# An audio tower with attention and a phase-table FFN: a ring of up to eight sequences in place of fixed quads, and softmax sums and squares on VectorE

## Chip, cores and metric

The kernel runs on one core of a Trainium2 chip. The metric is device time in microseconds. In this text PE is TensorE (PEld its weight loads), ACT is ScalarE, DVE is VectorE, POOL is GpSimd and SP is the engine that issues the DMAs.

## What is computed

The input is 32 signals, each cut into 313 frames of 512 samples. A DCT makes h; then come one attention layer and one FFN layer, each with a layernorm ahead and a residual around it. Everything is float32. Cut to what matters:

```python
h = frames @ D.T                                   # (32, 313, 512)
h = h + attn(layernorm(h))
h = h + ffn(layernorm(h))

# attn, 8 heads of 64
Q, K, V = rotate(X @ W_Q), rotate_inverse(X @ W_K), X @ W_V
p = softmax(Q @ K.T) * gamma_h ** abs(n - m)
Y = groupnorm(p @ V)                               # one group for each head
out = (silu(X @ W_G) * Y) @ W_O

# ffn, 256 units n, 512 features d
theta = x[..., None, :] / (1 + abs(W)) + B_param   # (32, 313, 256, 512)
idx = mod(round(theta * 4096 / (2 * pi)), 4096)
cos_sum = sum_d(cos_table[idx] * attn_cos)         # (32, 313, 256)
sin_sum = sum_d(sin_table[idx] * attn_sin)
out = silu(cos_sum @ proj_cos.T + sin_sum @ proj_sin.T)
```

The FFN is by far the largest part: 32 x 313 x 256 x 512 angles, of each a sine and a cosine.

## The kernel before, in words

**FFN** (`ffn`, line 538). The eight quads of four sequences are worked off one after the other. Features lie on the 128 partitions in four chunks c, and the 4 x 313 = 1252 frames of a quad along the free dimension, so a unit has 4 x 1252 = 5008 columns. For each of the 256 units DVE makes the table index: four instructions `index` (line 556), one for each chunk, multiply xT by the unit's scale and add its bias, both read per partition, and write int16; `mask` (line 563) wraps the index. ACT takes the sine of all 5008 columns in one instruction (line 581). For the cosine DVE adds a quarter turn (`quarter`, line 568) and wraps again (`wrap`, line 574), and ACT takes a second sine. PE sums over the features with one-hot weights `hot` (line 591): four sequences go to four groups of 32 output partitions of a PSUM bank, one row for each of 32 units. After 32 units DVE copies both banks (line 603) and SP stores them to `sums_d`. There are four index buffers, three sine buffers and four PSUM banks `pa`, of which a block of 32 units uses two.

**Attention** (`attention`, line 293) works on one sequence at a time: DCT (`rows`, line 275), layernorm with its reciprocal square root on POOL (lines 234 and 226), transposes, V, the gate's projection with silu (line 324), then two halves of four heads. For each pair of heads Q and K are projected twice (`columns`, line 289) and rotated on DVE. A half makes scores (line 352) and row maxima (line 360), and subtracts them for three heads (line 369); then ACT takes the exponentials with twelve instructions (line 378), each of which also gives the sum of its row block in `accum_out`. For every head follow transposes (399), the decay (411) and the product with V (417). At the end come the group norm (square on ACT, line 440; line 444 and on), the gate, W_O, the second layernorm and the store of the transposed result to `xT_d`. Copies of h, xnT, V and the last transposed block from PSUM are on ACT (line 210, `ENG_*`). `output` (line 493) loads the FFN sums of a sequence, projects them, takes the silu (510), adds h (513) and stores.

**Order.** The order on each engine is fixed before the run by `Plan` (line 46). Each operation has a key, an engine, an estimated duration and the buffers that it reads and writes; `emit` plays the engines forward and each takes, of what is ready, the operation with the lowest key. So keys say what is due first. An FFN unit takes two keys, one for each sine; a quad takes 512. The first four attentions run before any FFN, two at a time in buffer sets A and B (the memory of B is then given to the FFN by `swap`, line 692). Later attentions are spread over the FFN of the quad before (line 704), four in 452 keys, on buffer set A:

```python
    for b in range(QUAD):
        attention(plan, lambda x: -1000.0 + b // 2 + x, 0, b, (A, B)[b % 2])
    ...
    for q in range(n_quads):
        k0 = q * SLOTS
        for b in range(QUAD if q else 0):
            output(plan, k0 + 30.0 * b / QUAD - 4.0, q - 1, b, A)
        for b in range(QUAD if q + 1 < n_quads else 0):
            attention(plan, lambda x: k0 + 30.0 + (SLOTS - 60.0) * (b + x) / QUAD, q + 1, b, A)
        ffn(plan, k0)
```

Of the kernel before, what the change touches and what calls it, by code (L numbers as in the profile page):

```python
# [12 lines left out]
F32 = mybir.dt.float32  # L13
I32 = mybir.dt.int32
# [14 lines left out]
QUAD = 4  # L29
# [10 lines left out]
ENG_H = "ACT"  # L40
ENG_XNT = "ACT"
ENG_V = "ACT"
ENG_A5 = "ACT"
# [83 lines left out]
def tile_audio_tower(ctx: ExitStack, tc: tile.TileContext, t: dict, out: bass.AP):  # L127
    nc = tc.nc
    n_quads = t["frames"].shape[0]
    S = t["frames"].shape[4]  # L130
    T = QUAD * S
# [7 lines left out]
    out_v = out.rearrange("(a b) s d -> a b s d", b=QUAD)  # L139
# [8 lines left out]

    xT_d = dram.tile([P, NC4, T], F32, name="xT_d")
    sums_d = dram.tile([2, P, 2, T], F32, name="sums_d")  # L150
    wv_d = dram.tile([NC4, P, HOP], F32, name="wv_d")
    h_d = dram.tile([n_quads, QUAD, S, HOP], F32, name="h_d")

    class Buffers:


        def __init__(self, name, pool, psum):
# [8 lines left out]
            self.a5 = sb("a5", NC4, S)  # L166
            self.h = sb("h", NT, HOP)
            self.xn = sb("xn", NT, HOP)
            self.xnT = sb("xnT", NC4, S)
            self.v = sb("v", NT, HOP)  # L170
            self.gate = sb("gate", NC4, S)
            self.qk = [sb(f"qk{i}", 2, S) for i in range(2)]
            self.raw = sb("raw", 2, S)
            self.prob = sb("prob", NB, NT, S)
            self.probT = sb("probT", NT, S)
            wide = self.prob.rearrange("p a b s -> p (a b s)")
# [105 lines left out]
    def columns(plan, key, x, bank, src):  # L282

        k = x.load(plan, key, src)

        def go():
            w = x.ring[k].rearrange("p (c n) -> p c n", n=P)
            for c in range(NC4):
                nc.tensor.matmul(x.W[:, bank, :S], w[:, c, :], x.xnT[:, c, :],  # L289
                                 start=(c == 0), stop=(c == NC4 - 1))  # L290
        plan.add(key, "PE", 2200, go, (x.k("xnT"), x.k("ring", k)), x.banks(bank))

    def attention(plan, keys, q, b, x):
# [4 lines left out]
        def step(n=1.0):  # L298
            done[0] += n
            return keys(done[0] / 139.0)  # L300

        xns, probs = x.every("xn", NT), x.every("prob", NB)
        W3 = x.W[:N, :NT, :]
        plan.add(step(0), "SP", DMA_NS, lambda: nc.sync.dma_start(x.a5, t["frames"][q, b]), (),
                 (x.k("a5"),))
        rows(plan, step(7), x, x.a5, t["dct"], (x.k("a5"),))
        copy(plan, step(), ENG_H, NT * HOP, x.h[:N], W3, x.banks(0, 1, 2), (x.k("h"),))
        layernorm(plan, step(3), x)
        transposed(plan, step(3), x)
        copy(plan, step(), ENG_XNT, NC4 * S, x.xnT, x.W[:, :, :S], x.banks(0, 1, 2, 3), (x.k("xnT"),))  # L310
# [4 lines left out]
        copy(plan, step(), ENG_V, NT * HOP, x.v[:N], W3, x.banks(0, 1, 2), (x.k("v"),))  # L315
        plan.add(step(0), "POOL", 500, lambda: nc.gpsimd.memset(x.v[0:1, : NT - 1, :], 0.0), (),
                 (x.k("v"),))


        key = step(6)  # L320
        for g in range(NC4):
            columns(plan, key, x, g, t["wg"][g])
        plan.add(step(), "ACT", 1270,
                 lambda: nc.scalar.activation(x.gate, x.W[:, :, :S], AF.Silu),
                 x.banks(0, 1, 2, 3), (x.k("gate"),))

        for hb in range(H // NB):
            for g in range(hb * NB // 2, (hb + 1) * NB // 2):
                key = step(4)
                qk = x.qk[g % 2]  # L330
                kq = x.k("qk", g % 2)
# [12 lines left out]
                plan.add(key, "DVE", 1640, turned, x.banks(2, 3), (x.k("raw"), kq))  # L344
            for hd in range(hb * NB, (hb + 1) * NB):
                key = step(2.5)
                a, r0 = hd % NB, (hd % 2) * DH
                qk, kq = x.qk[hd // 2 % 2], x.k("qk", hd // 2 % 2)
# [25 lines left out]
            def exps(hb=hb, m=m):  # L374
                for a in range(NB):
                    for i in range(NT):
                        last = a == NB - 1
                        nc.scalar.activation(  # L378
                            x.prob[:N, a, i, :],
                            x.W[:N, i, :S] if last else x.prob[:N, a, i, :], AF.Exp,  # L380
                            bias=m[:N, i : i + 1] if last else 0.0,
                            accum_out=x.sm[:N, i, hb * NB + a : hb * NB + a + 1],
                        )

                nc.scalar.activation(x.lu[:1, 0:1], x.lu[:1, 0:1], AF.Silu)
            plan.add(step(), "ACT", 8700, exps, (x.k("mx", 1), *x.banks(0, 1, 2)),
                     [*probs, x.k("sm", hb), x.k("lu")])
            for hd in range(hb * NB, (hb + 1) * NB):
# [25 lines left out]
                for i in range(NT):  # L414
# [8 lines left out]
                    plan.add(key, "PE", 1000, go, (x.k("probT"), x.k("v")), x.banks(3))  # L423
                if hd % 2 == 0:
# [9 lines left out]


# [3 lines left out]
        plan.add(key, "ACT", 1500,  # L439
                 lambda: nc.scalar.activation(x.sq[:N], x.xn[:N], AF.Square), xns, probs)  # L440
# [23 lines left out]
        for c in range(NC4):  # L464
# [6 lines left out]
                 lambda: nc.vector.tensor_tensor(x.gate, x.gate, x.aff, ALU.mult), probs,  # L471
                 (x.k("gate"),))
        rows(plan, step(7), x, x.gate, t["wo"], (x.k("gate"),))
# [3 lines left out]
        for i in range(NT):  # L477
            f0 = 1 if i else 0
            plan.add(
                step(0), "SP", DMA_NS,  # L480
                lambda i=i, f0=f0: nc.sync.dma_start(
                    h_d[q, b, ROW0[i] + f0 : ROW0[i] + N, :], x.h[f0:N, i, :]),
                (x.k("h"),), (("h_d", q, b, i),),
            )
# [7 lines left out]

    def output(plan, key, q, b, x):

        probs, xns = x.every("prob", NB), x.every("xn", NT)

        def load():
            for m in range(2):
# [328 lines left out]
```

## Time and profile before

| | us |
|---|---|
| median of 3 runs | 19201.89 (19189.18 to 19209.79) |
| profiled execution | 19200.94 |
| its span, first to last instruction | 19199.2 |
| ACT busy, of it sines (line 581) | 18323.5, 17522.7 |
| DVE busy, of it index (line 556), mask, quarter, wrap (563, 568, 574) | 17754.5, 7108.7, 9010.3 |
| PE busy, of it the FFN's sums (line 591) | 14967.9, 10546.7 |
| first sine starts | 679.7 |
| last sine ends | 19130.4 |
| granted TensorE clock, mean | 0.913 |

A group line of the profile names source line, engine, operation, output and inputs, shapes and count; after the bar stand the busy time of the group in us and the mean duration in ns, and after the second bar the idle time of the engine just before these instructions, with what ended it. Instructions of one engine overlap a little in the records, so that the busy time of a group is less than count times mean. A line of the table of stretches gives for each engine its busy us and instructions in that stretch, then the granted clock as a share of full speed, the mean share of the DMA engines and GB/s.

### The profile page before, as it was taken

Reading aid. Unit: us, or ns where it says so; the run is one execution under the profiler, and the core shown is the slowest. Engines: PE = TensorE matmul, PEld = TensorE weight load, DVE = VectorE, ACT = ScalarE, POOL = GpSimd, SP = SyncE. Lnnn points to the kernel's source line nnn. Section 1 sums busy time; section 2 is a strip of 40 time slices with the busy share of each in tenths; the row PEclk is TensorE's granted clock in tenths of the full one; section 3 lists DMA queues with packets and bytes.
Section 4 is the critical chain, followed back from the end, with each engine's and each line's share of the span. In section 5 each row is a group of like instructions: output and inputs, shape, how many; then the busy total and the mean of one; then the engine's idle time right before and its main releaser. Section 6 shows DMA issues by size and latency. Waiting matters only on the chain.

```text
span 19199.2 us, 336270 instructions
## 1 busy us (share of the span) xinstructions
PE 14967.9 (78%) x148864; PEld 6732.7 (35%) x148864; DVE 17754.5 (92%) x17005; ACT 18323.5 (95%) x6051; POOL 581.0 (3%) x1222
## 2 busy tenths in 40 slices
PE   8777777887787877888777887788787777877666
PEld 5433333333333333333333333333333333322222
DVE  3799999999999999999999999999999999999997
ACT  1699999999999999999999999999999999999998
POOL 0000000000000000000000000000000000000000
PEclk8899999999999998999989999899999999987898
DMA  3111111111121111111111111111111111110001
GB/s 92 51 40 39 40 41 59 42 42 41 34 65 40 40 42 38 58 42 43 40 57 37 42 43 41 57 41 39 39 43 61 39 40 41 39 49 17 18 18 37
DMA packets 455954, 828.47 MB, mean 43 GB/s; under 512 B 54208, under 2 KB 103360, under 8 KB 454496
## 3 DMA queue, kind: packets, MB, share of 16 engines
q1 hardware_dynamic: 454496, 806.95, 14.3%
q8 instruction: 1169, 19.15, 0.4%
q14 instruction: 289, 2.37, 0.0%
HBM read 723.64 MB, written 83.10 MB: 42 GB/s over the span
## 4 chain that ended last, share of the span: by engine, by line
ACT 36%; DVE 33%; PE 17%; issue 11%; POOL 3%; DMA 0%; DVEq 0%; ACTq 0%; SPq 0%; POOLq 0%
ACT trig L581 34%; DVE ix L556 13%; PE pa L591 11%; DVE ix L563 5%; DVE ix L568 5%; DVE ix L574 5%; PE a_W L275 2%; PE a_W L289 2%; ACT a_prob L378 1%; DVE a_mx L360 1%; PE a_W L417 1%; PE a_W L352 1%; DVE a_prob L369 1%; POOL a_lu L226 1%; DVE a_st L238 0%
## 5 line engine op out<-in xcount | busy, mean ns | idle before, releaser
L581 ACT ACTIVATE trig<-ix 128x5008 f32<-128x5008 int16 x4096 | 17522.7, 4368 | 201.0 <-DVE ix L563 132.8
L591 PE MATMUL pa<-trig,hot 128*32 128x313 f32 x131072 | 10546.7, 468 | 3449.9 <-ACT trig L581 3433.5
L591 PEld LDWEIGHTS pa<-trig,hot 128*32 128x32 f32 x131072 | 4114.7, 117 | 9466.3 <-ACT trig L581 5200.6
L556 DVE TENSOR_SCALAR ix<-xT,f_scale,f_bias 128x1252 int16<-128x1252 f32 x8192 | 7108.7, 927 | 331.0 <-ACT trig L581 326.9
L568 DVE TENSOR_SCALAR ix<-ix 128x5008 int16<-128x5008 int16 x2048 | 3006.7, 1468 | 206.5 <-ACT trig L581 15.6
L563 DVE TENSOR_SCALAR ix<-ix 128x5008 int16<-128x5008 int16 x2048 | 2999.5, 1465 | 68.3
L574 DVE TENSOR_SCALAR ix<-ix 128x5008 int16<-128x5008 int16 x2048 | 3004.2, 1467 | 61.7
L289 PE MATMUL a_W<-a_xnT,a_ring 128*128 128x313 f32 x4800 | 1402.1, 437 | 92.2 <-DVE a_qk L338 66.6
L289 PEld LDWEIGHTS a_W<-a_xnT,a_ring 128*128 128x128 f32 x4800 | 873.3, 190 | 618.3 <-issue 156.1
L275 PE MATMUL a_W<-a_ring,a_a 128*105 128x512 f32 x1488 | 700.1, 612 | 27.5 <-DMA a_ring<-in_dct 15.4
L417 PEld LDWEIGHTS a_W<-a_v,a_probT 105*105 105x105 f32 x4320 | 482.7, 188 | 316.7 <-issue 187.5
L417 PE MATMUL a_W<-a_v,a_probT 105*105 105x64 f32 x4320 | 546.2, 277 | 41.1 <-DVE a_probT L411 41.0
L352 PE MATMUL a_W<-a_qk 64*105 64x313 f32 x1440 | 481.2, 459 | 100.8 <-DVE a_prob L369 75.9
L399 PE MATMUL a_W<-ident,a_prob 105*105 105x105 f32 x2160 | 350.4, 305 | 234.2 <-ACT a_prob L378 216.4
L275 PE MATMUL a_W<-a_ring,a_gate 128*105 128x512 f32 x720 | 377.0, 643 | 70.5 <-DVE a_gate L471 70.5
L399 PEld LDWEIGHTS a_W<-ident,a_prob 105*105 105x105 f32 x2160 | 282.0, 205 | 393.8 <-ACT a_prob L378 260.9
L275 PEld LDWEIGHTS a_W<-a_ring,a_a 128*105 128x105 f32 x1488 | 241.4, 173 | 419.4 <-issue 400.7
L275 PE MATMUL a_W<-a_ring,a_xnT 128*105 128x512 f32 x720 | 354.0, 616 | 2.8 <-ACT a_xnT L210 2.8
L226 POOL TENSOR_TENSOR a_gu<-a_gr 105x24 f32<-105x24 f32 x90 | 48.5, 539 | 10147.2 <-DVE a_gr L220 10142.5
L352 PEld LDWEIGHTS a_W<-a_qk 64*105 64x105 f32 x1440 | 224.1, 173 | 361.2 <-DVE a_prob L369 146.5
L262 PE MATMUL a_W<-ident,a_xn 105*128 105x105 f32 x1080 | 177.7, 291 | 172.5 <-DVE a_xn L250 90.1
L378 ACT ACTIVATE a_prob<-a_prob 105x313 f32<-105x313 f32 x540 | 242.6, 451 | 67.2 <-DVE a_prob L369 66.5
(136 smaller groups left out, 4029.3 us busy)
## 6 DMA issues: line engine op xcount, KB each, us to landing
hot<-in_hot SPq DMA_DIRECT2D x1024, 256.0 KB
a_dec<-in_decay SPq DMA_DIRECT2D x240, 260.5 KB
a_ring<-in_proj SPq DMA_DIRECT2D x128, 256.0 KB
a_ring<-in_dct SPq DMA_DIRECT2D x120, 256.0 KB
a_ring<-wv_d SPq DMA_DIRECT2D x120, 256.0 KB
a_ring<-in_wg SPq DMA_DIRECT2D x120, 256.0 KB
a_ring<-in_wq SPq DMA_DIRECT2D x120, 256.0 KB
a_ring<-in_wk SPq DMA_DIRECT2D x120, 256.0 KB
```

The costliest lines, as they stand in the source:

```text
L275: lambda c=c, i=i, k=k, to=to: nc.tensor.matmul(x.W[:N, to, :], lhsT[:, c, ROW0[i] : ROW0[i] + N], x.ring[k], start=(c == 0), stop=(c == N ...
L289: nc.tensor.matmul(x.W[:, bank, :S], w[:, c, :], x.xnT[:, c, :], start=(c == 0), stop=(c == NC4 - 1))
L352: lambda i=i, qk=qk, r0=r0: nc.tensor.matmul(x.W[:N, i, :S], qk[r0 : r0 + DH, 0, ROW0[i] : ROW0[i] + N], qk[r0 : r0 + DH, 1, :], start=Tru ...
L378: nc.scalar.activation(x.prob[:N, a, i, :], x.W[:N, i, :S] if last else x.prob[:N, a, i, :], AF.Exp, bias=m[:N, i : i + 1] if last else 0. ...
L399: nc.tensor.transpose(x.W[:N, jj, ROW0[i] : ROW0[i] + N], x.prob[:N, a, i, ROW0[j] : ROW0[j] + N], ident[:N, :N],)
L417: nc.tensor.matmul(x.y[:N, i, (hd % 2) * DH : (hd % 2 + 1) * DH], x.probT[:N, jj, ROW0[i] : ROW0[i] + N], x.v[:N, jj, hd * DH : (hd + 1) * ...
L556: nc.vector.tensor_scalar(now["ix", x][:, c, :], now["xT", c], f_scale[:, c, n : n + 1], f_bias[:, c, n : n + 1], ALU.mult, ALU.add)
L563: nc.vector.tensor_scalar(now["ix", x], now["ix", x], LUT - 1, LUT // 2, ALU.bitwise_and, ALU.bitwise_xor)
L568: nc.vector.tensor_scalar(new("ix", y, [P, NC4, T], I16, bufs=N_IX), now["ix", x], float(LUT // 4), None, ALU.add)
L574: nc.vector.tensor_scalar(now["ix", x], now["ix", x], LUT - 1, None, ALU.bitwise_and)
L581: nc.scalar.activation(new("trig", w, [P, NC4, T], bufs=N_TRIG), now["ix", x], AF.Sin, bias=-PI32, scale=ANG)
L591: nc.tensor.matmul(now["pa", p][b * 32 : b * 32 + 32, :S], now["hot", z][:, n % 2, c, k, :], now["trig", w][:, c, b * S : (b + 1) * S], st ...
```

## The change

**Ring and rounds.** Quads give way to 16 pairs of sequences. A ring has four places of one pair each. The FFN runs in 42 rounds of 32 units; a pair joins the ring at the round in `STARTS`, stays eight rounds, in which all 256 units come by (the block of units is the round's number modulo 8), and leaves. The ring holds one pair in rounds 0 to 3, two to round 9, three to round 13, four to round 35, then three, two and one for two rounds each. In rounds 36 and 37 the three pairs lie in places 0, 2 and 3, in rounds 38 and 39 the two lie in 0 and 2.

```python
STARTS = (0, 4, 8, 10, 12, 14, 16, 18, 20, 22, 24, 26, 28, 30, 32, 34)
SLOT = 16
```

**Width of an instruction.** Units are worked on two at a time. A sine instruction takes `n_p` parts (a part is one chunk of one unit, with all r sequences of the ring): eight with two sequences, four with four, two with six or eight. So a sine, mask, quarter or wrap again has 5008 columns, and 3756 with six sequences. An index instruction covers one part and one run of adjacent places of the ring: 626 columns for each pair in the run, 2504 with a full ring. With a full ring the sums take two banks for the sine and two for the cosine, which is all four.

```diff
-            for c in range(NC4):
-                def index(x=xs, c=c, n=n):
...
-                    nc.vector.tensor_scalar(
-                        now["ix", x][:, c, :], now["xT", c],
-                        f_scale[:, c, n : n + 1], f_bias[:, c, n : n + 1], ALU.mult, ALU.add)
+        n_p = min(SLOT // r, 2 * NC4) if SLOT % r == 0 else 2
+        E = n_p * r * S
+        n_slots = 2 * NC4 // n_p
+        n_banks = -(-r // 4)
...
+                        for pt, (c, u) in enumerate(parts):
+                            for at, j, m in runs:
+                                def index(x=x, pt=pt, c=c, u=u, n=n, at=at, j=j, m=m):
...
+                                    nc.vector.tensor_scalar(
+                                        now["ix", x][:, d0 : d0 + 2 * m * S],
+                                        now["xT", c][:, 2 * at * S : 2 * (at + m) * S],
+                                        f[:, 0, c, n + u : n + u + 1], f[:, 1, c, n + u : n + u + 1],
+                                        ALU.mult, ALU.add)
```

Scales and biases of the units no longer stay in SBUF: they are stored to DRAM (`f_d`) at the start, and each round loads its block of 32, eight keys ahead. With two sequences in a bank the even and odd units go to different partition groups, and the stores to `sums_d` are split in two.

**When attention runs.** Only the first two sequences run ahead of the FFN. The other thirty are spread by keys so that each pair is done eight keys before it joins: two of 60 keys, eight of 96, twenty of 128, the last ending at key 3448 of 4096. A joining pair is loaded into its place of the ring two keys ahead of the round. Outputs are placed between attentions, and the last two come after the last round.

**Exponentials, sums and squares.** `attention` gets an argument `eng`. It is "ACT" for the first two sequences and for those that start while the ring holds one pair (sequences 2, 3 and 4), and "DVE" for the other 27. With "DVE" the copies of h, xnT, V and the last transposed block are on DVE, and:

```diff
             def exps(hb=hb, m=m):
+                if eng == "DVE":
+                    nc.scalar.activation(x.prob[:N, : NB - 1], x.prob[:N, : NB - 1], AF.Exp)
                 for a in range(NB):
                     for i in range(NT):
                         last = a == NB - 1
-                        nc.scalar.activation(
...
-                            accum_out=x.sm[:N, i, hb * NB + a : hb * NB + a + 1],
-                        )
+                        if last or eng == "ACT":
+                            nc.scalar.activation(
...
+                                accum_out=x.sm[:N, i, hb * NB + a : hb * NB + a + 1]
+                                if eng == "ACT" else None,
+                            )
...
+            for a in range(0, NB if eng == "DVE" else 0, 2):
+                plan.add(step(0), "DVE", 2120,
+                         lambda h0=hb * NB + a, a=a: nc.vector.tensor_reduce(
+                             x.sm[:N, :, h0 : h0 + 2].rearrange("p i h -> p h i"),
+                             x.prob[:N, a : a + 2], AX.X, ALU.add),
...
+            plan.add(key, "DVE", 1760,
+                     lambda: nc.vector.tensor_tensor(x.sq[:N], x.xn[:N], x.xn[:N], ALU.mult),
```

**Buffers.** One buffer `u` serves as input frames, Q and K, gate, and last transposed block; V is written over h, so h is stored to DRAM after the DCT and loaded again after the heads; the gate's projection with its silu moves from ahead of the heads to behind them; `raw` is a part of `probT`. The four matmuls of `columns` become four operations of the plan in place of one.

## Prediction, made before the changed kernel ran

> **What bounds the kernel now.** I read the page's busy line first, then a table of stretches, then the groups of one steady quad by form.
>
> ```profile
> PE 14967.9 (78%) x148864; PEld 6732.7 (35%) x148864; DVE 17754.5 (92%) x17005; ACT 18323.5 (95%) x6051; POOL 581.0 (3%) x1222
> ```
>
> ACT is busy 95% and DVE 92%, so neither share alone names a bound. The stretches (columns: length, then busy us of PE, PEld, DVE, ACT, POOL, granted clock, DMA) separate four stages:
>
> ```profile
> 0.00:320.00 320.00, 274.47 (x1018) 187.69 (x1019) 117.58 (x144) 51.42 (x121) 13.12 (x58) 0.77 0.28 86
> 320.00:680.00 360.00, 305.41 (x1136) 200.19 (x1134) 131.33 (x194) 54.21 (x124) 21.70 (x100) 0.79 0.30 90
> ...
> 5367.30:7692.20 2324.90, 1847.42 (x18609) 829.75 (x18609) 2213.13 (x2124) 2289.80 (x757) 77.58 (x152) 0.93 0.15 44
> ...
> 17060.00:19060.00 2000.00, 1331.29 (x15016) 497.00 (x15008) 1844.16 (x1656) 2000.00 (x470) 0.00 (x0) 0.85 0.06 18
> ```
>
> Up to 680 us the first four attentions run alone, two at a time, with PE 85% busy and ACT nearly empty. A steady quad (four sequences of FFN with the next four attentions inside) takes 2324.9 us, 581 a sequence, with ACT at 98.5% and DVE at 95.2%; the last quad, without attention, runs ACT without a gap. After the last sine come 69 us of four output projections. The groups of the steady quad show what fills both engines (us in the stretch, mean ns, idle before):
>
> ```profile
> L581 ACT ACTIVATE trig<-ix 128x5008 f32<-128x5008 int16 x513 | 2195.5, 4367 | 28.1 <-DVE ix L563 17.7 <-DVE ix L574 7.0 <-PE pa L591 3.5
> L378 ACT ACTIVATE a_prob<-a_prob 105x313 f32<-105x313 f32 x72 | 32.3, 451 | 0.1
> L440 ACT ACTIVATE a_prob<-a_xn 105x1536 f32<-105x1536 f32 x4 | 5.9, 1466 | 0.0
> L210 ACT COPY a_v<-a_W 105x1536 f32<-105x1536 f32 x4 | 5.7, 1426 | 0.0
> ...
> L556 DVE TENSOR_SCALAR ix<-xT,f_scale,f_bias 128x1252 int16<-128x1252 f32 x1024 | 889.0, 927 | 31.5 <-ACT trig L581 31.2
> L568 DVE TENSOR_SCALAR ix<-ix 128x5008 int16<-128x5008 int16 x256 | 376.0, 1469 | 25.8 <-ACT trig L581 2.2 <-DVE ix L563 1.4
> ...
> L360 DVE TENSOR_REDUCE a_mx<-a_W 105x3 f32<-105x939 f32 x32 | 36.1, 1129 | 0.0
> L250 DVE TENSOR_SCALAR a_xn<-a_h,a_mv,a_lr 105x512 f32<-105x512 f32 x24 | 11.7, 543 | 17.5 <-POOL a_lr L229 17.5
> L444 DVE TENSOR_REDUCE a_gv<-a_prob 105x24 f32<-105x1536 f32 x4 | 7.0, 1746 | 0.0
> ```
>
> ACT waits 28 us for DVE and DVE 31 us for ACT: they are balanced, and a change pays only if it relieves both. PE waits for the sines.
>
> **Units.** A *slot* is one full sine (5008 columns), 4.27 us from start to start (ten in 42.8 us near the end). One key of the plan is one slot, and the work has 4096 of them before and after. A *pair* (sine and cosine of the same indices) needs on DVE the index instructions plus mask, quarter and wrap: 4.40 us (1126.4/256). Four index instructions take 3.45 us together, so 0.841 from start to start and 0.086 at the end. Against L250 (same form, 512 columns) the slope is (927-543)/740 = 0.520 ns a column, leaving 0.190 us fixed. So 626 columns cost 0.516, 1878 cost 1.167, 2504 cost 1.492.
>
> DVE per pair: eight sequences 2x1.492+0.09+4.40 = 7.47; four 7.85, as now; two 8x0.516+0.09+4.40 = 8.61; six (0.75 of the width, the three int16 steps 1.141 each) 2.42+3.42 = 5.84.
>
> Attention and output on DVE sum to 232.9 us in that quad, 58.2 a sequence. Calibration: 64x7.85+58.2+1.9 (part copies) = 562.5 against 581.0, so 18.5 are gaps and waits, of which 31.2/4 = 7.8 are waits for ACT and 10.7 stay even when DVE is the limit.
>
> **ACT per sequence.** Three heads' exponentials: nine starts of 0.448 become one of 2.44 (slope 0.832 from the L440 and L378 durations, less the 0.09 overlap that the sines show); the fourth head loses its sum reads (3x0.50 to 3x0.40). That is 1.9 twice, 3.8. Copies moved: 1.43+1.42+1.19+1.18 = 5.2. Square 1.47. Together -10.4; ACT falls from 572.4 to 562.0.
>
> **DVE per sequence.** Four sums of 1878 columns: between L360 and L444 1.03 ns a column, 2.10 each, 8.4. Square as a product: 1.75 (fp32 products of 1536 take that). Copies from PSUM: two of 1.75, two of 1.46, 6.4. Together +16.6. Against it stand the merged index instructions, -0.38x64 = -24.
>
> Here a rule of the Trainium skill speaks against the change. "VectorE: DVE Perf Modes", section on the TRN2 errata, prices a VectorE SBUF instruction at 58 cycles plus its columns, so 0.060 us fixed at its 0.96 GHz (and says of itself that it is too low). By the rule merging saves 0.120x64 = 7.7 a sequence, less than the 16.6 added; by the row 24.3. I take the row: it is this very instruction at two sizes.
>
> **The sum by stage.** The order of the changed kernel puts attentions 2 and 3 in keys 0 to 120, eight more at 96 keys each to 888, and twenty at 128 keys each to 3448, where DVE's order indeed has them.
>
> *Start.* Two attentions, not four. The last copy of the first pair starts at 341.8, of the second at 655.3, 24.5 before the first sine (679.7). The new loads are half as large, the first index group longer: 22. First sine at 364.
>
> *Keys 0-120* (ring of one pair, ACT still does copies and sums): DVE 30x8.61+58.2+0.9+10.7 = 328 a sequence, ACT 283. DVE is the limit. PE: 60 slots of 2.55 plus 136 for an attention ((1847-1303)/4, 1303 being the FFN's) is 289, 88%. No row shows attention at this density: 656 if PE hides, 800 if the chain through PE gives 400 each. I add 2%, as the start shows PE feeding two attentions at 85%: 669.
>
> *Keys 120-888.* First one, still on ACT: 48x7.85+3+58.2+1.4+10.7 = 450. Three at four sequences: 376.8+58.2+16.6+1.4+10.7 = 464, 1391. Four at six: 64x5.84+58.2+16.6+1.9+10.7 = 461, 1845. ACT needs only 426 to 429: DVE bound. Sum 3686.
>
> *Keys 888-3448.* DVE 64x7.47+58.2+16.6+1.9+18.5 = 573.3, ACT 562.0+8.7 idle = 570.7. The larger, twenty times: 11,466 (581 each before).
>
> *Keys 3448-4096.* Eight wide: 264x4.27 = 1127. Six: 256 sines of 3.23 = 826. Four and two stand in separate places of the ring, so 626-column pieces: 8.77 a pair with 0.16 of dependent gaps, above ACT's 8.54: 561+281. Outputs 13. Sum 2808.
>
> *End.* Before, the second sequence's silu starts 33.5 after the last sine; with its add and store 41, not 69.
>
> 364+669+3686+11,466+2808+41 = 19,034; with 1.7 around the span 19,036. The same working gives 19,209 for before, where 19,199 was measured, and the median of runs lies 1 us above that execution. Counted at nothing, with the cover named: the second store and the reload of h (96 SP issues each; queued behind them on SP are weights fetched three ahead, and the next reader of h comes a third of an attention later; uncovered, 3.2 us as the sums' load takes at the end, 32 times, 102); the f blocks of a round, fetched 8 keys ahead (uncovered 3.2x42 = 134); the gate's projection, now behind the heads (attention is paced by keys, not by its own length); xT of a joining pair (three of four chunks are read for the last time a pair or more before the round ends, and the first is free three pairs early). In wide rounds all four PSUM banks are in use, so a round's first matmul waits for DVE's copies of the last one, and DVE's copy for PE, with index work queued behind it: 0.48 each, covered by three sine buffers; else up to 4 us in each of 22 rounds, 90. None can gain.
>
> **Rivals.**
> 1. *The gaps close.* With larger instructions, more of them independent neighbours, DVE runs without its 10.7: keys 0-120 635, to 888 3600, then 565x20; total about 18,750. For: an independent neighbour hides the 0.1 us before L568. Against: each pair still has its own dependent chain, and waits for POOL (17.5 in the quad before L250) remain.
> 2. *The early chain binds.* Attention at half the former time waits through PE, and the queue behind each waiting DVE instruction with it; pair 1 joins late: 400 a sequence twice (+131) and 4 more on eight (+32): 19,200, no change. For: PE 88%. Against: the order is interleaved for it. Here the ring doesn't do what it says.
> 3. *Slower: DVE in the wide rounds.* Merging pays only the rule's 60 ns: +0.26 a pair, 16.6 a sequence, 333 there, little net elsewhere: about 19,350. It decides from a 2504-column index of 1.57 us start to start. Against: the two sizes of one form.
>
> **How the numbers follow.** Forecast 0.64 (18,890 to 19,160), rival 1 0.14, rival 2 0.15 (about half within the bound, the rest below it), rival 3 0.07. A measurement can tell 0.2%, 38 us. Faster 0.64+0.14+0.08 = 0.86, same 0.07, slower 0.07. The range, 18,870 to 19,175, leaves out rival 3, most of the lower case of rival 1 and what lies above 19,175 in rival 2.
>
> **What would show it.** First sine near 364; 2504-column index near 1.58 long; steady sequence 573; ACT idle around 7% before the wide rounds with DVE still near 95%, so that ACT's share of the span doesn't rise though its work falls by some 270. Wrong if the steady sequence stays at 581, if joins show ACT waiting for tens of microseconds, or if the first pairs' rounds exceed 700.

## The result, and the profile after

| | before | changed |
|---|---|---|
| median of 4 runs, us | 19195.53 (19188.64 to 19209.79) | 18894.07 (18891.78 to 18913.65) |
| profiled execution, its span | 19200.94, 19199.2 | 18894.1, 18892.3 |
| granted TensorE clock, mean | 0.913 | 0.926 |

The ratio is 0.9844 [0.9827, 0.9861]: 1.6% faster, at 18,894 us where 19,036 was forecast. In the changed kernel the index instruction is line 610, mask, quarter and wrap are 622, 630 and 636, the sine is 643, the sums' matmul 664 and the copy of the sums from PSUM 681. The busy line of its page:

```profile
PE 14803.3 (78%) x148864; PEld 6590.0 (35%) x148864; DVE 17770.2 (94%) x15244; ACT 18090.3 (96%) x5026; POOL 656.5 (3%) x1222
```

ACT has 233 us less work, DVE as much as before (+16), in 1761 fewer instructions. The table of stretches, cut at the sines that open a stage (start, up to the last copy of the first two attentions; keys 0 to 120; 120 to 504; 504 to 888; 888 to 3448, called the wide stage below, since the ring is full in nearly all of it; 3448 to 4096):

```profile
0.00:309.00 309.00, 267.47 (x1065) 177.40 (x1066) 129.58 (x169) 50.06 (x121) 17.77 (x82) 0.85 0.36 109
331.00:981.30 650.30, 529.47 (x4794) 269.40 (x4795) 612.18 (x803) 562.38 (x239) 31.30 (x64) 0.89 0.21 62
981.30:2819.50 1838.20, 1497.23 (x14527) 697.20 (x14529) 1760.76 (x1718) 1718.93 (x493) 87.36 (x157) 0.93 0.17 52
2819.50:4658.50 1839.00, 1482.41 (x14496) 670.85 (x14488) 1753.37 (x1646) 1720.51 (x573) 76.45 (x151) 0.95 0.15 46
4658.50:16033.40 11374.90, 9182.30 (x92944) 4076.65 (x92944) 10883.33 (x8246) 11245.01 (x2880) 440.42 (x760) 0.93 0.13 40
16033.40:18848.40 2815.00, 1805.87 (x20940) 684.52 (x20940) 2618.68 (x2646) 2788.01 (x721) 3.15 (x10) 0.91 0.08 24
```

Up to key 888 DVE is busy 94 to 96% and ACT less: DVE is the limit. In the wide stage, twenty sequences of 568.7, it is the other way round: ACT is busy 98.9% (562.3 a sequence) and DVE 95.7% (544.2). Before, in 13,920 us of steady quads, a sequence had 572.4 of ACT work and 8.5 of idle.

Where the time went. For the kernel of before the keys are priced at its 4.534 us a key beside attention (seven quads in 16,251.3), the last quad as measured:

| stage | before, us | changed, us | difference |
|---|---|---|---|
| to the first sine | 679.7 | 331.0 | -348.7 |
| keys 0 to 888 | 4026.5 | 4327.4 | +300.9 |
| keys 888 to 3448 | 11,608.0 | 11,374.9 | -233.1 |
| keys 3448 to 4096 | 2816.1 | 2815.0 | -1.1 |
| after the last sine | 68.8 | 43.9 | -24.9 |
| sum | 19,199.1 | 18,892.2 | -306.9 |

The early start is nearly all given back in the next 888 keys, where ten attentions lie closer together than DVE can carry at 4.53 us a key; the wide stage makes 233 of the net 307 us. The changed kernel's groups by form (whole span):

```profile
L643 ACT ACTIVATE trig<-ix 128x5008 f32<-128x5008 int16 x3520 | 15061.8, 4365 | 324.7 <-PE pa L664 144.4 <-DVE ix L622 91.5 <-DVE ix L636 52.0
L379 ACT ACTIVATE a_prob<-a_prob 105x2817 f32<-105x2817 f32 x54 | 138.0, 2555 | 0.6
...
L610 DVE TENSOR_SCALAR ix<-xT,f 128x2504 int16<-128x2504 f32 x2816 | 4345.9, 1581 | 189.6 <-ACT trig L643 189.1
...
L610 DVE TENSOR_SCALAR ix<-xT,f 128x626 int16<-128x626 f32 x1536 | 833.2, 603 | 16.5 <-ACT trig L643 10.8 <-DMA xT<-xT_d 0.2
L610 DVE TENSOR_SCALAR ix<-xT,f 128x1878 int16<-128x1878 f32 x512 | 623.3, 1257 | 3.0 <-ACT trig L643 3.0
...
L397 DVE TENSOR_REDUCE a_sm<-a_prob 105x6 f32<-105x1878 f32 x108 | 222.5, 2102 | 0.0
```

The index takes 603, 1257 and 1581 ns at 626, 1878 and 2504 columns: the straight line through the rows of before, with a fixed part that merging saves. The sums take the 2.10 us that were forecast.

### The profile page after: what moved, and what is told of

Same layout as the page of the kernel before. It is cut to its first block, busy times and chain, and to the rows that moved or that the text cites. A ratio compares the mean times of both kernels' runs of the same rounds, so it can differ in the third digit from the quotient of the medians.

```text
span 18892.3 us, 332980 instructions
## 1 busy us (share of the span) xinstructions
PE 14803.3 (78%) x148864; PEld 6590.0 (35%) x148864; DVE 17770.2 (94%) x15244; ACT 18090.3 (96%) x5026; POOL 656.5 (3%) x1222
## 4 chain that ended last, share of the span: by engine, by line
DVE 55%; ACT 18%; PE 15%; issue 8%; POOL 3%; DMA 1%; DVEq 0%; SPq 0%; ACTq 0%; POOLq 0%
DVE ix L610 20%; ACT trig L643 18%; DVE ix L630 9%; DVE ix L622 9%; PE pa L664 8%; DVE ix L636 8%; PE a_W L288 3%; PE a_W L273 2%; DVE a_mx L363 1%; DVE a_prob L372 1%; DVE a_sm L397 1%; DVE a_probT L424 1%; DVE a_st L236 1%; PE a_W L355 1%; POOL a_lu L224 1%
## 5 line engine op out<-in xcount | busy, mean ns | idle before, releaser
L643 ACT ACTIVATE trig<-ix 128x5008 f32<-128x5008 int16 (+1 forms) x4288 | 17547.6, 4178 | 442.0 <-PE pa L664 185.5
L610 DVE TENSOR_SCALAR ix<-xT,f 128x2504 int16<-128x2504 f32 (+3 forms) x5888 | 6673.8, 1184 | 211.9 <-ACT trig L643 205.8
L630 DVE TENSOR_SCALAR ix<-ix 128x5008 int16<-128x5008 int16 (+1 forms) x2144 | 3014.4, 1406 | 201.2 <-DVE ix L622 5.0
L622 DVE TENSOR_SCALAR ix<-ix 128x5008 int16<-128x5008 int16 (+1 forms) x2144 | 3023.7, 1410 | 69.2
L636 DVE TENSOR_SCALAR ix<-ix 128x5008 int16<-128x5008 int16 (+1 forms) x2144 | 3017.3, 1407 | 67.2
L273 PE MATMUL a_W<-a_ring,a_u 128*105 128x512 f32 x2256 | 1101.5, 623 | 120.8 <-DVE a_u L499 53.7
L430 PE MATMUL a_W<-a_h,a_probT 105*105 105x64 f32 x4464 | 540.6, 270 | 118.0 <-DVE a_probT L424 117.7
L273 PEld LDWEIGHTS a_W<-a_ring,a_u 128*105 128x105 f32 x2256 | 360.2, 174 | 722.8 <-issue 579.0
L430 PEld LDWEIGHTS a_W<-a_h,a_probT 105*105 105x105 f32 x4464 | 476.3, 181 | 386.4 <-issue 194.7
L355 PE MATMUL a_W<-a_u 64*105 64x313 f32 x1488 | 502.8, 466 | 112.0 <-DVE a_prob L372 100.6
L363 DVE TENSOR_REDUCE a_mx<-a_W 105x3 f32<-105x939 f32 x248 | 280.2, 1130 | 17.7 <-PE a_W L355 17.1
L424 DVE TENSOR_TENSOR a_probT<-a_W,a_dec 105x939 f32<-105x939 f32 x248 | 279.9, 1129 | 13.0 <-PE a_W L412 13.0
```

The costliest lines, as they stand in the source:

```text
L273: lambda c=c, i=i, k=k, to=to: nc.tensor.matmul(x.W[:N, to, :], lhsT[:, c, ROW0[i] : ROW0[i] + N], x.ring[k], start=(c == 0), stop=(c == N ...
L355: lambda i=i, qk=qk, r0=r0: nc.tensor.matmul(x.W[:N, i, :S], qk[r0 : r0 + DH, 0, ROW0[i] : ROW0[i] + N], qk[r0 : r0 + DH, 1, :], start=Tru ...
L363: lambda m=m: nc.vector.tensor_reduce(m[:N], x.W[:N, :NT, :S], AX.X, ALU.max),
L430: nc.tensor.matmul(x.y[:N, i, (hd % 2) * DH : (hd % 2 + 1) * DH], x.probT[:N, jj, ROW0[i] : ROW0[i] + N], x.v[:N, jj, hd * DH : (hd + 1) * ...
L610: nc.vector.tensor_scalar(now["ix", x][:, d0 : d0 + 2 * m * S], now["xT", c][:, 2 * at * S : 2 * (at + m) * S], f[:, 0, c, n + u : n + u + ...
L622: nc.vector.tensor_scalar(tl, tl, LUT - 1, LUT // 2, ALU.bitwise_and, ALU.bitwise_xor)
```

## Experiments

The stage of keys 888 to 3448 as each run with the ring shows it, us a sequence, and the whole (medians). The kernel of before was run again beside these runs, at medians of 19191.8 to 19198.6, so a difference of less than some 7 us between two totals says nothing.

| kernel | length | ACT busy, idle | DVE busy, idle | whole |
|---|---|---|---|---|
| before (steady quads) | 581.0 | 572.4, 8.5 | 553.3, 27.7 | 19195.53 |
| changed | 568.7 | 562.3, 6.5 | 544.2, 24.6 | 18894.07 |
| e1_all_act | 578.7 | 572.0, 6.6 | 530.6, 48.0 | 19063.26 |
| e2_wide_only | 569.4 | 562.8, 6.6 | 543.4, 26.0 | 18875.26 |
| e3_no_merge | 586.8 | 563.4, 23.4 | 567.4, 19.4 | 19349.22 |
| e5_copies | 577.5 | 567.6, 9.9 | 536.2, 41.4 | 19070.43 |
| e6_sums | 571.6 | 566.9, 4.7 | 539.0, 32.6 | 18928.08 |
| e7_columns | 567.7 | 562.3, 5.4 | 544.1, 23.6 | 18852.32 |
| e8_best | 569.6 | 562.8, 6.7 | 543.4, 26.2 | 18878.97 |
| x1_in_block | 572.6 | 565.9, 6.7 | 544.8, 27.8 | 18970.47 |
| x2_apart | 571.5 | 565.7, 5.8 | 544.6, 26.9 | 18958.30 |
| e11_best | 568.4 | 562.8, 5.5 | 543.3, 25.1 | 18838.19 |

Busy time here is the profile's. Where an expectation below gives ACT's idle time (3 for the changed kernel, 8 for before), ACT's semaphore instructions, into whose record part of a wait falls, had been counted as busy (565.5 us a sequence in the changed kernel with them, 562.3 without); by the profile's count these are 6.5 and 8.5. The fall that the later expectations set out to explain was thus 2, not 5.

**e1_all_act: the ring alone.** No work moves from ACT to DVE.

```diff
-            plan, lambda x: k + (e - k) * x, 2 + i, A, "ACT" if narrow else "DVE")))
+            plan, lambda x: k + (e - k) * x, 2 + i, A, "ACT")))
```

> The changed kernel with copies, sums, exponentials and squares left on ACT for all 32 sequences (ring and merged index instructions alone). Load theory (each stage takes the fuller engine's work plus about 3 us of ACT idle for a wide sequence): wide sequence 565.9+10.4+2.9 = 579 (568.7 in the changed kernel), 20 times +210; the seven narrow-round sequences that were on DVE lose 16.6 us of DVE work but meet ACT at about 446, -95; total 19,010. Handoff theory (ACT starves because of its own instructions that wait in the attention chain, 8.1 us idle a sequence as before): wide 584, total 19,110. DVE the limit everywhere: 27x16.6 less, 18,450.

Measured: 19063.26 (19058.4 to 19072.79), 0.9934 [0.9919, 0.9949]. The wide sequence is 578.7, as the load theory gave it; the total misses its 19,010 by 53, since unloading DVE in the rounds of four and six sequences gained some 30 us and not 95. Its wide stage (the changed kernel's stands above):

```profile
4621.80:16194.90 11573.10, 9223.03 (x92944) 4115.67 (x92944) 10612.55 (x8064) 11440.92 (x3780) 420.91 (x758) 0.93 0.13 39
```

ACT is busy 98.9%, just as in the changed kernel, with 196 us more work; the stage is 198 longer. In the wide rounds the offload is worth what it takes from ACT, and DVE's 271 us more cost nothing.

**e2_wide_only: the offload only with a full ring.**

```diff
-        narrow = sum(q is not None for q in rings[int(np.searchsorted(key_of, k, "right")) - 1]) <= 1
+        narrow = sum(q is not None for q in rings[int(np.searchsorted(key_of, k, "right")) - 1]) <= 3
```

> The changed kernel, with the move to DVE only for sequences that start while the ring holds four pairs (ACT keeps the work for all ten before). Load theory: DVE is the limit from key 216 to 888, so that stretch falls from about 460 to about 446 a sequence where ACT's 437 meets it; -95, total 18,800, wide sequences unchanged at 569. Rival (the narrow rounds are bound by the attention's chain through PE): no change, 18,890.

Measured: 18875.26 (18869.65 to 18881.47), 0.9836 [0.9821, 0.985]: 19 better than the changed kernel, not the 94 expected. Keys 216 to 504 fell from 1383.3 to 1353.9, keys 504 to 888 only from 1838.9 to 1834.2. The stretch of these last keys:

```profile
2787.20:4621.40 1834.20, 1488.06 (x14524) 679.34 (x14516) 1702.43 (x1618) 1758.03 (x753) 81.87 (x154) 0.95 0.16 47
```

DVE lost 12.7 us of work a sequence, ACT gained 9.4, and the length fell by 1.2: with DVE at 93% and ACT at 96% each now waits for the other (33 and 19 us a sequence). Near balance, a microsecond taken from one engine isn't a microsecond of time.

**e3_no_merge: index instructions never cover more than two pairs.** The full ring then takes two of 1252 columns where the changed kernel takes one of 2504.

```diff
-            if runs and runs[-1][0] + runs[-1][2] == at:
+            if runs and runs[-1][0] + runs[-1][2] == at and runs[-1][2] < 2:
```

> The changed kernel with index instructions of at most two places of the ring (1252 columns). Load theory with the fixed cost of 0.190 us from the two sizes: DVE +0.38 a pair, 24 us a wide sequence, which makes DVE the limit at about 592 (568.7): +465, and +97 in the rounds of six; total 19,450. With the page's 60 ns of fixed cost: +7.7 a wide sequence, DVE hardly over ACT: 18,950 to 19,050.

Measured: 19349.22 (19340.44 to 19352.33), 1.0082 [1.0067, 1.0097]: slower than before. Groups of its stage of keys 888 to 3448, DVE's, then ACT's:

```profile
L610 DVE TENSOR_SCALAR ix<-xT,f 128x1252 int16<-128x1252 f32 x5116 | 4440.2, 928 | 2.8 <-ACT trig L643 2.7
```

```profile
L643 ACT ACTIVATE trig<-ix 128x5008 f32<-128x5008 int16 x2552 | 10930.8, 4364 | 441.3 <-DVE ix L622 322.9 <-DVE ix L636 76.2 <-PE pa L664 35.5
```

DVE hardly waits for a free index buffer any more (2.7 us in twenty sequences, 82 in the changed kernel), and ACT waits 399 us for indices: here DVE is the limit. It has 23.2 us more work a sequence than in the changed kernel (24 forecast), and the sequence is 18.0 longer; that is 5 short of the 592 expected, since DVE had some room in the changed kernel, and the total is 100 below the 19,450. By the 0.060 us of the rule in the prediction the work would have grown by 7.7, so the fixed 0.190 us of the row is about right, and the merge is what makes room for the offload.

**e4_before_offload: the offload in the kernel of before**, with its quads and 1252-column indices: copies, merged exponentials, sums and squares as in the changed kernel for the 28 sequences beside the FFN.

```diff
...
-            attention(plan, lambda x: k0 + 30.0 + (SLOTS - 60.0) * (b + x) / QUAD, q + 1, b, A)
+            attention(plan, lambda x: k0 + 30.0 + (SLOTS - 60.0) * (b + x) / QUAD, q + 1, b, A, "DVE")
```

> The kernel before (quads) with copies, sums, exponentials and squares as in the changed kernel for the 28 sequences beside the FFN. Load theory: DVE 553+16.6 with some 20 of gaps becomes the limit, 590 or more a sequence (581): +260 at least, 19,460 to 19,650. Rival (relief of ACT pays by itself): -10.4 a sequence, 18,905.

Measured: 19458.19 (19454.74 to 19464.56), 1.0139 [1.0122, 1.0156], at the lower edge of what the load theory gave (19,460 to 19,650). Its quads take 2362 to 2365 us after the first, 590.8 a sequence. A stretch of them:

```profile
5300.00:14700.00 9400.00, 7379.10 (x74024) 3324.49 (x74028) 9035.64 (x8593) 8968.12 (x2293) 328.34 (x608) 0.92 0.15 44
```

DVE is busy 96.1% and ACT 95.4%: DVE has become the limit. The offload alone costs 1.4%, the ring alone saves 0.7%, together they save 1.6%.

**e5_copies and e6_sums: the offload in halves.** e5 moves only the four copies to DVE, e6 everything but the copies.

```diff
# e5_copies
-                if eng == "DVE":
+                if False:
                     nc.scalar.activation(x.prob[:N, : NB - 1], x.prob[:N, : NB - 1], AF.Exp)
...
-            for a in range(0, NB if eng == "DVE" else 0, 2):
+            for a in range(0, 0, 2):
...
-        if eng == "ACT":
+        if True:
# e6_sums, and so for xnT, V and the last transposed block
-        copy(plan, step(), eng, NT * HOP, x.h[:N], W3, x.banks(0, 1, 2), (x.k("h"),))
+        copy(plan, step(), "ACT", NT * HOP, x.h[:N], W3, x.banks(0, 1, 2), (x.k("h"),))
```

> The changed kernel with only the four copies on DVE; exponentials with their sums and the square stay on ACT. Load theory: wide ACT 565.9+5.3+2.9 = 574, +108 over twenty; narrow sequences lose 10.2 of DVE work, about -65; total 18,935. If the exponentials' blocks on ACT are what starves it, idle goes back to 8: 19,035.

> The changed kernel with the four copies back on ACT; exponentials, sums and square as changed. Load theory: wide ACT 565.9+5.2+2.9 = 574, +106; narrow -6.4 of DVE work, about -45; total 18,955. If the copies' waits for PE are what starves ACT, its idle time goes back to 8: 19,055.

Measured: e5 19070.43 (19061.52 to 19075.39), 0.9932 [0.9917, 0.9947]; e6 18928.08 (18927.1 to 18932.49), 0.9859 [0.9844, 0.9874]. So e6 lies 27 below its load theory, while e5 lies 135 above its 18,935, nearer to the 19,035 for blocks of exponentials that starve ACT; x1 and x2 below test that. With e1 (neither half moved) and the changed kernel (both) there are two readings of each half. Moving the copies takes 4.4 to 4.6 us of ACT work a sequence but shortens it by 1.2 (e1 to e5) or 2.9 (e6 to changed); ACT's idle time takes the rest back. Moving exponentials, sums and squares takes 5.2 to 5.3 and shortens it by 7.1 (e1 to e6) or 8.8 (e5 to changed). Over the whole kernel the copies give nothing or 34 us (e5 against e1: +7; changed against e6: -34), the other half 135 to 176.

**x1_in_block and x2_apart: is it the length of the block of exponentials?** Both keep the changed kernel's work and add two copies of 939 columns for each half, to a tile that nothing reads: x1 inside the block of exponentials (whose estimated duration in the plan rises by as much), x2 between other ACT work.

```diff
# x1_in_block, in exps
+                if eng == "DVE":
+                    for _ in range(2):
+                        nc.scalar.copy(x.extra[:N], x.xnT[:N, :NT, :])
# x2_apart, behind every second head
+                if hd % 2 and eng == "DVE":
+                    plan.add(key, "ACT", 880,
+                             lambda: nc.scalar.copy(x.extra[:N], x.xnT[:N, :NT, :]),
+                             (x.k("xnT"),), (x.k("extra"),))
```

> The changed kernel with two additional copies of 939 columns (0.88 us each, into a scratch tile) inside each block of exponentials, for the 27 sequences with sums on DVE: ACT has 3.5 us more a sequence, and its longest stretch without a sine goes from 6.4 back to about 8.2 us. Block theory (DVE fills its four index buffers while ACT takes exponentials, then waits, and ACT starves for the time lost): ACT idle in a wide sequence rises from 3.2 to about 7, wide sequence 576, total 19,040. Rival (only the sum of work counts): idle stays 3.2, wide 572.2, total 18,965.

> The same additional copies, four a sequence, but each by itself between sines (in the heads' second part), not in the block. Both theories: ACT idle stays about 3.2, wide sequence 572.2, total 18,965. If it comes out as x1_in_block, the block's length has no part in it.

Measured: x1 18970.47 (18966.98 to 18974.08), 0.9883 [0.9868, 0.9898]; x2 18958.3 (18949.62 to 18964.49), 0.9878 [0.9861, 0.9894]. ACT's work rises by 3.7 and 3.4 a sequence, its idle time by 0.2 and -0.7. Two blocks that are 3.7 us longer together are paid with 3.9, no more: the block theory falls. In these two, as between e1 and the changed kernel, an ACT microsecond in the wide rounds is about a microsecond of time; the copies of e5 are the exception, and stay open below.

**e7_columns: the four matmuls of a Q or K projection as one operation of the plan**, as before the change.

```diff
-        w = x.ring[k].rearrange("p (c n) -> p c n", n=P)
-        for c in range(NC4):
-            plan.add(
-                key, "PE", 550,
-                lambda c=c: nc.tensor.matmul(x.W[:, bank, :S], w[:, c, :], x.xnT[:, c, :],
-                                             start=(c == 0), stop=(c == NC4 - 1)),
-                (x.k("xnT"), x.k("ring", k)), x.banks(bank),
-            )
+        def go():
+            w = x.ring[k].rearrange("p (c n) -> p c n", n=P)
+            for c in range(NC4):
+                nc.tensor.matmul(x.W[:, bank, :S], w[:, c, :], x.xnT[:, c, :],
+                                 start=(c == 0), stop=(c == NC4 - 1))
+        plan.add(key, "PE", 2200, go, (x.k("xnT"), x.k("ring", k)), x.banks(bank))
```

> The changed kernel with the four matmuls of a projection as one operation of the plan again. If the finer order on PE shortened the first two attentions (first sine at 331, 364 was forecast), the first sine moves to 345 or later and the total by +15 to +30. If a higher granted TensorE clock in the first 310 us did it, the first sine stays within 5 us of 331 and the total at 18,894.

Measured: 18852.32 (18851.26 to 18853.1), 0.9819 [0.9803, 0.9835]: 42 better than the changed kernel, and the first sine at 325.7 (331.0), so the finer order did not shorten the start: the kernels with the finer order, whose starts are alike, show first sines from 324 to 336. Half of the 42 is in the wide rounds. ACT's waits there (line, waited for: us, times, longest), first of the changed kernel, then of e7, whose lines are two lower:

```profile
ACT trig L643 <- PE pa L664: 54.1, 26, 3.8
ACT trig L643 <- DVE ix L636: 32.6, 30, 2.7
ACT a_xn L531 <- PE a_W L273: 20.2, 9, 3.8
...
ACT trig L643 <- DVE ix L622: 7.8, 12, 3.9
```

```profile
ACT trig L641 <- PE pa L662: 32.3, 27, 2.9
ACT trig L641 <- DVE ix L634: 29.4, 30, 2.7
ACT a_xn L529 <- PE a_W L273: 18.2, 9, 3.9
ACT trig L641 <- DVE ix L620: 10.1, 21, 3.9
```

The sine waits 22 us less for PE to free a sine buffer; the stage is 21 shorter. So the finer order of the projections was a small cost of the change; that its matmuls slip in ahead of the FFN's sums is the likely way, not one that was followed in the trace.

**e8_best: the ring's last pairs in neighbouring places**, on top of e2, so that the index of the rounds with two pairs covers 1252 columns.

```diff
-                at = min((a for a, q in enumerate(ring) if q is None), key=lambda a: -sum(
-                    0 <= y < len(ring) and ring[y] is not None for y in (a - 1, a + 1)))
+                at = max((a for a, q in enumerate(ring) if q is None), key=lambda a: (rd > 0) * (4 * sum(
+                    0 <= y < len(ring) and ring[y] is not None for y in (a - 1, a + 1)) + a) - (rd == 0) * a)
```

> As e2_wide_only, and places of the ring chosen so that the two pairs left in rounds 38 and 39 are neighbours (index instructions of 1252 columns in place of two of 626). Load theory: the 128 keys there fall from 4.37 to 4.28 a key, -11: about 18,790. Rival (the last rounds are bound by something else): as e2_wide_only.

Measured: 18878.97 (18876.78 to 18881.47), 0.9833 [0.9818, 0.9848], e2's time again. Keys 3904 to 4032, first of e2, then of e8:

```profile
17981.60:18540.90 559.30, 382.38 (x4136) 143.33 (x4136) 547.39 (x710) 552.32 (x131) 0.00 (x0) 0.86 0.10 29
```

```profile
17995.80:18552.60 556.80, 357.44 (x4136) 137.87 (x4136) 510.83 (x467) 549.47 (x132) 0.00 (x0) 0.90 0.10 29
```

DVE has 37 us less to do, and the stretch is 2.5 shorter: ACT is busy 99% of it in both and is the limit, so the separate pieces cost 2.5 us at most and not the 11 expected.

**e10_before_gate: the gate's projection behind the heads, in the kernel of before.** This asks for the start, which was 33 us shorter than forecast.

```diff
-        key = step(6)
-        for g in range(NC4):
-            columns(plan, key, x, g, t["wg"][g])
...
+        key = step(6)
+        for g in range(NC4):
+            columns(plan, key, x, g, t["wg"][g])
```

> The kernel before with the gate's projection and silu behind the heads, as in the changed kernel. If that order shortened the first two attentions (last copy of the first pair at 341.8 before, 308.9 in the changed kernel), it comes at 330 or earlier here, with the first sine before 660 and the total about 19,170. If the granted clock did it, the copy comes later than 335 unless the clock of the first 300 us is above 0.80, and the total stays at 19,195.

Measured: 19233.25 (19223.98 to 19243.8), 1.002 [1.0011, 1.0028]; the quads are 7 to 14 us longer each, so that the whole is slower, where 19,170 or 19,195 was expected. The first pair of attentions comes to its end (start of the last copy of a transposed block) at 330.4, at 341.8 before and at 308.9 in the changed kernel. Stretches to that point, of before, then of e10 (the changed kernel's stands in the table above):

```profile
0.00:341.80 341.80, 288.37 (x1065) 194.62 (x1065) 129.46 (x169) 52.62 (x122) 17.76 (x82) 0.78 0.30 92
```

```profile
0.00:330.40 330.40, 287.89 (x1064) 193.77 (x1064) 129.40 (x169) 50.12 (x121) 17.77 (x82) 0.78 0.31 95
```

PE is busy 87% in e10 and in the changed kernel (309.0 us), over the same number of matmuls; busy time by clock is 287.9 x 0.78 = 225 and 267.5 x 0.85 = 227, the same work. PE's idle time tells the two causes apart: 53 us before, 43 in e10 and 42 in the changed kernel. So the gate's place gives 11 of the 33 us, and PE's shorter busy time at the higher granted clock some 21. The clock moves the start without any change of order, too: e4, whose gate stands where it stood before, also comes to this point at 330.6, with 51 us of PE idle time but 279 busy at a clock of 0.80, and the kernels with the ring range from 302 (clock 0.87) to 314 (0.84). Why the clock differs no run shows.

**e11_best: e2 and e7 together.**

> e2_wide_only and e7_columns together: ACT keeps copies, sums, exponentials and squares until the ring is full, and a projection's four matmuls are one operation of the plan. If the two gains add: 18,894-19-42 = 18,833. If both come from the same waits in the narrow rounds: 18,850.

Measured: 18838.19 (18834.51 to 18840.12), 0.9814 [0.9799, 0.9829]: the gains add (18,833 was expected). It is the fastest version, 56 us below the changed kernel.

## Why the prediction was right, and where its sizes were off

The sign was right, and so was the mechanism: the early start is given back while DVE is the limit up to key 888, the offload pays in the wide stage, and the merged index instructions make room for it. Wrong was which engine limits the wide stage: DVE was forecast, and it is ACT. The time lies 142 us (0.75%) below the forecast, about midway to rival 1's 18,750.

| term | forecast | measured | miss |
|---|---|---|---|
| start | 364 | 331.0 | -33 |
| keys 0 to 120 | 669 | 650.2 | -19 |
| keys 120 to 888 | 3686 | 3677.2 | -9 |
| keys 888 to 3448 | 11,466 | 11,374.9 | -91 |
| keys 3448 to 4096 | 2808 | 2815.0 | +7 |
| end | 41 | 43.9 | +3 |

**Work.** ACT's work in a wide sequence was forecast at 562.0 and measured 562.3. DVE's 554.8 counts from start to start; the same count for before, 562.5, stood against 553.3 of busy time, so busy time should be 545.6: 544.2 was measured. Of its parts the offload was put too high, at 16.6 of DVE's time, where e1 and the changed kernel differ by 13.5 of busy time. Between the profile's row for the index instruction and the rule of 58 cycles that the prediction set against it, the row was right: e3 shows that without the wide merge a sequence is 18 us longer. What rival 3 feared, DVE overfull in the wide rounds, is what e3 and e4 show; the changed kernel escapes it by the merge.

**The mis-sized term: DVE's 18.5 of "gaps and waits".** The wide stage was put at the larger of DVE's 554.8 + 18.5 = 573.3 and ACT's 562.0 + 8.7 = 570.7. But a part of the 18.5 were waits for ACT, 7.8 by the prediction's own count: idle time of an engine that was not the limit, which is no load. Where DVE is the limit the same count of work leaves much less: 325.1 - 317.4 = 7.7 in keys 0 to 120, 461.1 - 453.0 = 8.1 in keys 216 to 504, 459.7 - 450.5 = 9.2 to 888, and 586.8 - 579.1 = 7.7 in e3. For the early stages 10.7 had been kept, which is 6 us too much before key 120 and some 14 from there to 888. With 7.7 DVE's side of the wide stage is 562.5; ACT's, 570.7, is the larger, and 568.7 came. Of the 91 us, 52 came from taking the wrong side of the two, and about 40 from ACT's idle time, 6.5 and not 8.7. That the stage came within 0.8% was luck in part: the two sides lay 2.6 apart, so that the wrong one cost little.

**ACT's idle time: what went and what came.** Sorting ACT's waits by their distance from the copies that end a round (nearer than 20 us or not), before had 154 us of waits elsewhere in 24 sequences, 6.4 each, and the changed kernel 45 in 20, 2.3 each; e1 has 2.6, so this came with the ring and its larger index instructions, not with the offload. But at the round's end the changed kernel loses 75 us in 20 rounds, 3.8 each, and so a sequence; before it was 1.0 for each end of a 32-unit block, of which a sequence had two. So the 8.7 carried over from before stood for two parts, and they moved in opposite directions. The prediction had priced the end of a round, "up to 4 us in each of 22 rounds", and had counted it at nothing, as covered by three sine buffers. As far as the four PSUM banks alone go that holds: at key 3584 the ring is full and all four banks change hands, but no attention is left, and ACT does not wait at all. The stretch of 25 us on both sides of it (ACT busy 50.00 of 50; DVE, at 45, has more room than in the wide stage):

```profile
16599.60:16649.60 50.00, 36.13 (x384) 13.09 (x376) 45.01 (x34) 50.00 (x12) 0.00 (x0) 0.80 0.08 22
```

At key 3712, the next end, ACT waits 0.2 us. What isn't covered is the attention that begins at the ends before these. The timeline of the changed kernel around one end of a round (start, length, engine, line; in brackets the idle time before, and who ended it):

```profile
8103.87 5.40 PE L273 MATMUL a_W<-a_ring,a_u 128*105 128x512 f32 x12
...
8104.95 0.87 DVE L681 COPY part<-pa 128x313 f32<-128x313 f32 x2
...
8109.20 6.53 PE L664 MATMUL pa<-trig,hot 128*32 128x313 f32 x96
...
8111.63 12.91 ACT L643 ACTIVATE trig<-ix 128x5008 f32<-128x5008 int16 x3 [2.93 <-PE pa L664]
...
8115.69 1.58 DVE L610 TENSOR_SCALAR ix<-xT,f 128x2504 int16<-128x2504 f32 x1
8115.86 1.46 POOL L224 TENSOR_TENSOR a_lu<-a_lr 105x3 f32<-105x3 f32 x1 [46.79 <-DVE a_lr L218]
...
8117.30 1.47 DVE L622 TENSOR_SCALAR ix<-ix 128x5008 int16<-128x5008 int16 x1
8117.40 1.42 POOL L225 TENSOR_TENSOR a_lu<-a_lu,a_lv 105x3 f32<-105x3 f32 x1
8118.87 1.47 DVE L630 TENSOR_SCALAR ix<-ix 128x5008 int16<-128x5008 int16 x1
8118.90 1.49 POOL L226 TENSOR_SCALAR a_lu<-a_lu 105x3 f32<-105x3 f32 x1
...
8120.47 0.19 POOL L227 TENSOR_TENSOR a_lr<-a_lr,a_lu 105x3 f32<-105x3 f32 x1
...
8122.91 1.46 DVE L248 TENSOR_SCALAR a_xn<-a_h,a_mv,a_lr 105x512 f32<-105x512 f32 x3 [2.57 <-POOL a_lr L227]
...
8124.28 1.46 DVE L636 TENSOR_SCALAR ix<-ix 128x5008 int16<-128x5008 int16 x1
...
8125.86 4.38 ACT L643 ACTIVATE trig<-ix 128x5008 f32<-128x5008 int16 x1 [1.31 <-DVE ix L636]
```

PE gives the next attention's DCT 5.4 us in one piece, while DVE copies the banks, and only then frees three sine buffers in a burst of 96 matmuls; ACT has stood for 2.93. Soon after, DVE waits 2.57 for POOL's reciprocal root, the indices are queued behind that layernorm, and ACT stands for 1.31. Attention begins every 128 keys and so do the rounds, so both fall on one spot. At every second end a pair also leaves the ring, and its outputs are due: 20 of the 75 us are their silu, waiting for its own projection on PE (`a_xn L531` in e7's list above). How the rest divides between the DCT, the layernorm and their meeting with the banks was not separated, and a shift of the attention against the round was not tried.

**Start.** Forecast by halving before's; 11 of the 33 us are the gate's place, which the prediction counted at nothing because keys pace attention; the first two, however, run ahead of the FFN, at their own pace. The other 21 come with the clock, for which the prediction has no term. **Keys 0 to 120:** 13 us of the miss are the 2% added for PE; rival 2's chain through PE does not show, PE was busy 81%. **Keys 3448 to 4096:** the 561 for the rounds with two pairs came out at 559.3, but by luck: DVE's 626-column pieces were to be the limit there, and e8, without them, still takes 556.8. **What was to show it:** ACT idle 6 to 7% in keys 216 to 888 with DVE at 95 to 96%, as forecast. ACT's share of the span rose a little, from 95.4 to 95.8%, where it was not to rise; its work fell by 233 us and not 270.

**Left open:** why ACT's idle time in the wide rounds is 9.9 in e5, 6.5 in the changed kernel and 4.7 in e6, with ACT's work nearly equal in e5 and e6. The block's length is ruled out by x1 and x2. In e6 nearly all of it (87 of 95 us) lies at the round's end, in e5 less than half (78 of 198), so what differs lies between the ends.

## What to carry to other kernels

When two engines are both near full, take each one's busy time in the stage and add only the gaps that it shows where it is itself the limit; idle time of the other engine is not a load that can be carried over. Moving work from the fuller engine to the other pays only after room has been made there: here the same offload cost 1.4% alone and saved 0.9% after the merge. And work placed at regular keys is better not begun where a round's end already takes every PSUM bank and a burst of PE: ends without it cost nothing here, ends with it 3.8 us, though no run moved it.

## What the runs showed of the hardware that was not expected

Small POOL operations depend on what DVE does meanwhile. In the timeline above 105x3 operations took 1.42 to 1.49 us beside DVE's instructions on the index (L610, L622, L630), each ending just after the DVE instruction did, and 0.19 us as soon as DVE stood (8120.47). Over the whole changed kernel 204 of the 768 such operations took more than 0.4 us, all of them beside DVE, and the 551 that met no DVE instruction took 0.19 to 0.20. The Trainium skill ("GPSIMD Engine Reference", section 1, Specifications) says that the two engines share their SBUF interfaces and contend when DVE runs in a two-port mode or reads two SBUF inputs; the rows show the contention, but not the mode that DVE ran in. The price here is a layernorm whose POOL chain is drawn out by the very indices that are queued behind it: DVE waits 5.1 us a sequence for it (102 us in the wide stage). DVE is not the limit there, so what this costs in time no run shows.

The granted TensorE clock up to the end of the first two attentions was 0.78 to 0.80 in the kernels with quads (before, e4, e10) and 0.84 to 0.87 in those with the ring, for the same matmuls (1064 or 1065) at a busy share of 84 to 88%. No run explains it.
